# A graph layer and a layer of 64 experts on one core: the aggregation matrix from products of 32 by 128 instead of 64 by 64, thirteen instead of eleven experts' weights on chip, and a reordered transition and end

## The chip, the cores and the metric

The kernel runs on one core of a Trainium2 chip. A core has a matrix engine (TensorE, "PE" in the profile; "PEld" is its loading of weights, which overlaps it), a vector engine (VectorE, DVE), a scalar engine (ScalarE, ACT), a general engine (GpSimd, POOL) and a queue engine (SyncE, SP) that issues DMAs. Each works through its own instructions in order, and semaphores order them between engines. SBUF is the on-chip memory of 128 partitions, PSUM the accumulators that TensorE writes. The metric is the device time of one execution in microseconds: before the change 466.25 us, the median of three runs (465.24 to 466.73).

## The reference

There are 1024 tokens (nodes) of 512 values and 16384 edges sorted by destination.

```
x = x + relu(segment_sum(edge_val * (layernorm(x) @ W)[edge_col], edge_row) + bias)   # here row = src, col = dst
nx = layernorm(x)
scores = sigmoid(nx @ Wg.T + bg); w, idx = top_k(scores, 2); w = w / w.sum()           # 64 experts
h1 = (gamma_e * nx + beta_e) @ W1_e + b1_e      # 512 -> 256, per expert
h3 = (gamma_e * nx + beta_e) @ W3_e + b3_e
y  = sum over the two chosen experts of w_e * (silu(h1) * h3) @ W2_e + b2_e
z  = (silu(nxs @ Ws1 + bs1) * (nxs @ Ws3 + bs3)) @ Ws2 + bs2,  nxs = nx * gs + bs      # shared expert, width 32
out = x + y + z
```

Everything is fp32. The call passes the sorted `src` and `dst` in the edge places, as the first line is written above. The experts' matrices are 64 x 1.57 MB (W1, W3 and W2 of 512 KB each), some 100 MB that have to be read once.

## The kernel before, in words

**Graph layer.** The 1024 by 1024 aggregation matrix is built densely. The nodes of the sorted side are cut into 256 windows of DL = 4 nodes, in NH = 2 halves of 128 windows. A window's edges (up to 128, one a partition) are described by two one-hot matrices: one tells, for each edge, node-in-window times HI plus the high part of the other node's number, and the other, scaled by the edge's weight, its low part. With LO = 64 low and HI = 16 high values both have 64 columns, and their fp32 product (line 485) is the window's 64 by 64 piece of the matrix. NS = P / LO = 2 products go side by side into the two halves of the PSUM partitions. `one_hots` makes both one-hots for 16 windows, a group: VectorE compares (lines 398 and 400) and multiplies by the weight (401), ScalarE turns the first into fp32 (399). `matrix_group` makes the 16 products of a group and has ScalarE copy the accumulator, in two copies, into the tiles A (490). `turn` transposes A on TensorE (498), and ScalarE copies the result scaled by `sure` into AT (501). `weighted_sum` multiplies AT with the rows of layernorm(x) W (507). There are eight groups for each half; beside the second half's groups TensorE turns the first half's and begins the weighted sums of three tiles.

A fallback for edges that do not fit their window, in a branch, is not taken with these inputs, and its two loads of the flag (`unsure_i`) only hold up the engines a moment.

**Finishing and routing.** A loop over the 8 tiles of 128 tokens sums, normalizes, stores `nx_d` in device memory for the gathers, computes scores, chooses two experts (`choose`), ranks the tokens within each expert (`rank`, `put`) and marks slots and expert pairs (`slots`, `listed`). The result is `lists` and `tokens`: for each of 32 pairs of experts 64 + 64 slots with row numbers (691 and 692).

**Expert blocks.** 33 blocks: 32 expert pairs and, at place 24 of the order, a block for one expert's overflow beyond 64 tokens. The schedule is written by hand. For each block `gather` fetches 128 rows on POOL's queue (717), `scaled` transposes and applies gamma and beta (729, 731), `hidden` adds the biases by two pairs of bf16 matmuls (742: a pair for the high and middle terms and a pair for the low one) and does 16 fp32 matmuls for the pair, two experts side by side in the columns (746), then silu on ScalarE (749) and the product on VectorE (751), `turned`, `outputs` (768, 771), and a scatter of the block's 128 rows to `y_d` on POOL's queue (775). `outputs` of a block come after the hidden matmuls of the next one. Weights are loaded on SP's queue in the order W1, W3, W2 of each expert (703, 704, 706). They go to two rings of AHEAD = 11 slots: "w13" of 8 KB a partition and "w2" of 4 KB. Many tiles of the earlier stages are put in the same rings (`big` and `mid`: one-hots, A, AT), so that a weight load has to wait until the tile that had the slot is done with. Other tiles (rows, windows, transposed h) are in the pools `graph` and `graph2`.

Before the first block POOL zeroes four row buffers, four gathers are issued, and `weights` and the shared expert of two tiles (`other_rows`, `other_turn`, `other_sum`) are computed; the six other tiles follow from block 13 on. `beyond` and the functions after it make the overflow lists in blocks 2 to 12.

**End.** The last block is not scattered. `y_d` is read back in eight loads (1006) on the ACT and SP queues, the two rows of each token are multiplied by their weights and added to the result on VectorE (1014), and the last block's part comes from a one-hot matmul (`block_hots`, 1010) that VectorE adds (1016). Half of the first rows are added on TensorE with diagonal matrices instead.

## Time and profile before

| what | from | value |
|---|---|---|
| median of 3 runs | times | 466.25 us |
| the profiled execution | times | 467.33 us |
| its span, first to last instruction | page | 465.5 us |
| mean granted TensorE clock | page | 0.962 |
| busy: PE, PEld, DVE, ACT, POOL | page | 422.5, 210.6, 233.5, 112.0, 116.2 us |
| moved by DMA | page | 132.48 MB, 285 GB/s over the span |
| matrix phase, first to last product group | trace | 46.0 to 94.2 us |
| finishing loop's weighted sums end | trace | 165.4 us |
| first hidden matmul | trace | 191.2 us |
| last weights on chip | trace | about 431.8 us |

A profile is of one execution, and lies here 1.08 us above the median of the runs; 1.83 us of it are outside the span. A group of instructions is written as: line, engine, operation, output<-input, shape, count, then busy time, mean ns of one, and the idle time of the engine just before them with what ended it. A matmul that overlaps the next has a mean longer than its share of the time, so the pace is read from the starts. An fp32 matmul appears as two records with a weight load each. Times on POOL are rough.

### The profile page before, as it was taken

The page shows a single profiled execution, that of the slowest core. Times are in us where ns is not written, and L with a number is a line of the kernel's source. Part 1 is how long each engine was busy: PE and PEld are TensorE (multiplying, and loading weights), DVE is VectorE, ACT ScalarE, POOL GpSimd, SP SyncE. Part 2 cuts the span into 40 slices and gives each one's busy share as a digit, 9 for nine tenths or more (in the row PEclk, how much of TensorE's full clock was granted, in tenths as well). Part 3 has the DMA queues.
Part 4 walks back from the last instruction along what each step waited for, and adds up shares of the span by engine and source line. Part 5 has one row for each costly group of instructions (what it writes and reads, how often), then busy time and mean ns, then how long its engine had stood idle before and what let it go on. Part 6 is the DMA issues. An engine that isn't in the chain of part 4 may idle for free. (4 is left out here: it accounts for less than half of the span.)

```text
span 465.5 us, 6433 instructions
## 1 busy us (share of the span) xinstructions
PE 422.5 (91%) x2182; PEld 210.6 (45%) x2182; DVE 233.5 (50%) x690; ACT 112.0 (24%) x240; POOL 116.2 (25%) x148
## 2 busy tenths in 40 slices
PE   2999999987999964996999999999999999999781
PEld 1554996754555543332434434333333443434230
DVE  6879996036877875428424333233233232412265
ACT  1335785324121212011111212112121121212200
POOL 6542200000432124312223233232232322200200
PEclk9999999998999985799899999999999999999988
DMA  8286830360786195359999999999999999999194
GB/s 263 87 121 102 321 130 3 125 259 28 244 316 204 52 375 195 121 194 410 356 389 407 407 407 406 407 408 405 408 404 409 406 405 407 405 410 403 47 366 174
DMA packets 42294, 132.48 MB, mean 285 GB/s; under 512 B 8023, under 2 KB 8151, under 8 KB 42128
## 3 DMA queue, kind: packets, MB, share of 16 engines
q1 hardware_dynamic: 30464, 107.56, 59.7%
q0 software_dynamic: 8304, 18.17, 13.3%
q10 hardware_dynamic: 3488, 6.30, 3.7%
q8 instruction: 18, 0.29, 0.3%
q14 instruction: 20, 0.16, 0.1%
HBM read 124.00 MB, written 18.88 MB: 307 GB/s over the span
## 5 line engine op out<-in xcount | busy, mean ns | idle before, releaser
L746 PE MATMUL xph<-w,xT 128*64 128x512 f32 (+1 forms) x520 | 126.5, 602 | 0.9 <-DMA w<-in_L_ffn_W_dram 0.9
L775 POOL DMA_INDIRECT y_d<-xy,lists x31 | 31.9, 1030 | 169.8 <-ACT xhT L760 70.4
L746 PEld LDWEIGHTS xph<-w,xT 128*64 128x64 f32 (+1 forms) x520 | 39.0, 138 | 66.6 <-issue 63.6
L768 PE MATMUL xpy<-w,xhT 128*64 128x512 f32 (+1 forms) x260 | 67.0, 593 | 0.6 <-ACT xhT L760 0.6
L751 DVE TENSOR_TENSOR xh<-xa,xph 128x256 f32<-128x256 f32 x33 | 13.9, 421 | 106.8 <-ACT xa L749 106.8
L507 PE MATMUL acc<-hw,AT 128*128 128x512 f32 x128 | 61.5, 607 | 0.0
L749 ACT ACTIVATE xa<-xph 128x256 f32<-128x256 f32 x33 | 12.6, 383 | 152.1 <-PE xph L746 152.1
L717 POOL DMA_INDIRECT rows<-nx_d,tokens x32 | 35.5, 1109 | 12.4 <-issue 9.1
L768 PEld LDWEIGHTS xpy<-w,xhT 128*64 128x64 f32 (+1 forms) x260 | 21.5, 138 | 37.2 <-issue 35.1
L485 PEld LDWEIGHTS ph<-oh 128*64 128x64 f32 x512 | 31.7, 212 | 5.7 <-issue 3.3
L485 PE MATMUL ph<-oh 128*64 128x64 f32 x512 | 33.3, 302 | 0.1
L297 PE MATMUL ph<-w_sb,hT 128*128 128x512 f32 x64 | 30.5, 625 | 0.7 <-ACT hT L290 0.7
L771 ACT COPY xy<-xpy 128x512 f32<-128x512 f32 x33 | 19.3, 586 | 49.0 <-PE xpy L768 44.1
L729 DVE TENSOR_TENSOR xT<-xpt,gT 128x512 f32<-128x512 f32 x32 | 22.0, 687 | 16.7 <-PE xpt L194 15.3
L507 PEld LDWEIGHTS acc<-hw,AT 128*128 128x128 f32 x128 | 22.3, 193 | 17.4 <-issue 17.4
L731 DVE TENSOR_TENSOR xT<-xT,bT 128x512 f32<-128x512 f32 x32 | 22.2, 693 | 1.1
L607 POOL TENSOR_SCALAR so<-rank_at,here 128x128 f32<-128x128 f32 x14 | 8.9, 634 | 54.5 <-DVE here L598 54.5
L194 PE MATMUL xpt<-ident,rows 128*128 128x128 f32 x132 | 22.3, 296 | 0.0
L401 DVE TENSOR_TENSOR oh<-eq,wt 128x1024 f32<-128x1024 bf16 x16 | 19.6, 1224 | 3.6 <-PE pt L498 2.2
L194 PEld LDWEIGHTS xpt<-ident,rows 128*128 128x128 f32 x132 | 19.5, 211 | 1.1 <-issue 0.6
L758 PEld LDWEIGHTS xpht<-ident,xh 128*128 128x128 f32 x66 | 11.8, 216 | 16.1 <-DVE xh L751 7.0
L297 PEld LDWEIGHTS ph<-w_sb,hT 128*128 128x128 f32 x64 | 12.4, 203 | 14.1 <-issue 13.1
(275 smaller groups left out, 493.9 us busy)
## 6 DMA issues: line engine op xcount, KB each, us to landing
w<-in_L_ffn_W_dram SPq DMA_DIRECT2D x195, 512.0 KB
y_d<-zero POOLq DMA_DIRECT2D x1, 4096.0 KB
base_d<-in_L_gnn_bias_dram POOLq DMA_DIRECT2D x1, 2048.0 KB, 19.9
base<-base_d POOLq DMA_DIRECT2D x8, 256.0 KB, 13.3
nx_d<-nx ACTq DMA_DIRECT2D x8, 256.0 KB
ys<-y_d ACTq DMA_DIRECT2D x4, 512.0 KB
ys<-y_d SPq DMA_DIRECT2D x4, 512.0 KB
w_sb<-in_L_gnn_W_dram ACTq DMA_DIRECT2D x1, 1024.0 KB
```

The costliest lines, as they stand in the source:

```text
L194: nc.tensor.transpose(ps[:, k, :], v[:, k, :], ident[:n, :n])
L297: nc.tensor.matmul(ph, hT[:, k, :], w_sb[:, k, :], start=(k == 0), stop=(k == KC - 1))
L401: nc.vector.tensor_tensor(oh[:, 1], eq[:, 1], wt[:, h, None, q].to_broadcast([P, LO, 16]), ALU.mult)
L485: nc.tensor.matmul(pa[LO * w:LO * (w + 1), u, :], oh[:, 1, :, q], oh[:, 0, :, q], start=True, stop=True)
L507: nc.tensor.matmul(accs[t], ATs[h][t // 4][:, t % 4, wq, :], hws[h][:, wq, :], start=(h == 0 and wq == 0), stop=(h == NH - 1 and wq == NQ ...
L717: nc.gpsimd.indirect_dma_start(out=rows, out_offset=None, in_=nx_d[:, :], in_offset=bass.IndirectOffsetOnAxis(ap=of, axis=0), bounds_check ...
L729: nc.vector.tensor_tensor(xT.rearrange(view, n=n), pt.rearrange(view, n=n), g[:, :, :, None].to_broadcast(over), ALU.mult)
L731: nc.vector.tensor_tensor(xT.rearrange(view, n=n), xT.rearrange(view, n=n), b[:, :, :, None].to_broadcast(over), ALU.add)
L746: nc.tensor.matmul(ph[n * r:(n + 1) * r], xT[:, k, n * r:(n + 1) * r], w13[:, :, k, :], start=False, stop=(k == KC - 1))
L768: nc.tensor.matmul(py[n * r:(n + 1) * r], hT[:, c, n * r:(n + 1) * r], w2[:, c, :], start=(c == 0), stop=(c == HC - 1))
L771: nc.scalar.copy(y, py)
L775: nc.gpsimd.indirect_dma_start(out=y_d[:, :], out_offset=bass.IndirectOffsetOnAxis(ap=numbers, axis=0), in_=y, in_offset=None, bounds_chec ...
```

## The change

The line numbers of the kernel after differ, so parts are named by function.

1. `LO` becomes 32, so HI = 32 and NS = 4: a product is 32 by 128, and four go side by side. The first one-hot has 128 columns, of which ScalarE casts 96 and VectorE writes 32 directly; the second has 32 columns. `turn` transposes four contiguous slices. The window numbering follows.
2. `AHEAD` becomes 13. To make room, the pools `graph` and `graph2` give up most tiles to the two rings: three "w2" slots hold the ring of row tiles and one the transposed h until routing ends, and the overflow lists take one (`room`).
3. The biases become three bf16 terms stacked on 96 partitions, so that one pair of matmuls adds them; the loads of b1 and b3 become 12.
4. The routing chain: the bias matmul of the scores goes first, part of `put` goes to `choose`, the making of `rank_at` goes behind the matrix loop, `weights` goes behind the first block's hidden matmuls, all eight tiles' shared expert goes into the blocks from 6 on, ScalarE zeroes three row buffers in place of POOL's four, and three gathers are issued ahead.
5. The end: the last pair's W1 and W3 are loaded before its W2s; `y_d` is read back on SP's queue, issued ahead of the last block's hidden matmuls; the last two blocks are not scattered but added by one-hot matmuls, interleaved with the additions.

```
-AHEAD = 11
+AHEAD = 13
...
-    LO = 64
+    LO = 32
...
+    EH = E // 2
+    bias3 = const.tile([3 * EH, 2, 2 * H], BF16, name="bias3")
+    picks = const.tile([3 * EH, 2, E], BF16, name="picks")
...
+        row_ring = [pair[:, j] for pair in [mid([P, 2, D], "row", F32) for _ in range(3)] for j in range(2)]
+        turned_ring = mid([P, 2, KC, P], "hT", F32)
...
-                eq = mid([P, 2, LO, 16], "eq", BF16)
-                oh = big([P, 2, LO, 16], "oh")
-                nc.vector.tensor_tensor(eq[:, 0], iv, vl[:, 0, h, None, q].to_broadcast([P, LO, 16]), ALU.is_equal)
-                nc.scalar.copy(oh[:, 0], eq[:, 0])
-                nc.vector.tensor_tensor(eq[:, 1], iv, vl[:, 1, h, None, q].to_broadcast([P, LO, 16]), ALU.is_equal)
-                nc.vector.tensor_tensor(oh[:, 1], eq[:, 1], wt[:, h, None, q].to_broadcast([P, LO, 16]), ALU.mult)
-                return oh
+                v, low = vl[:, 0, h, None, q], vl[:, 1, h, None, q]
+                eq = mid([P, VA, 16], "eq", BF16)
+                ov = big([P, P, 16], "ov")
+                ol = mid([P, 2, LO, 16], "ol", F32)
+                eql = ol[:, 1].rearrange("p l q -> p (l q)").bitcast(BF16)[:, :LO * 16].rearrange("p (l q) -> p l q", q=16)
+                nc.vector.tensor_tensor(eq, iv[:, :VA], v.to_broadcast([P, VA, 16]), ALU.is_equal)
+                nc.scalar.copy(ov[:, :VA], eq)
+                nc.vector.tensor_tensor(eql, iv[:, :LO], low.to_broadcast([P, LO, 16]), ALU.is_equal)
+                nc.vector.tensor_tensor(ol[:, 0], eql, wt[:, h, None, q].to_broadcast([P, LO, 16]), ALU.mult)
+                nc.vector.tensor_tensor(ov[:, VA:], iv[:, VA:], v.to_broadcast([P, P - VA, 16]), ALU.is_equal)
+                return ov, ol[:, 0]
...
-                        nc.tensor.matmul(pa[LO * w:LO * (w + 1), u, :], oh[:, 1, :, q], oh[:, 0, :, q],
+                        nc.tensor.matmul(pa[LO * w:LO * (w + 1), u, :], ol[:, :, q], ov[:, :, q],
                                          start=True, stop=True)
...
+            def score_bias(t):
+                pls[t] = psh.tile([P, D], F32, name="ph")[:, :P]
+                nc.tensor.matmul(pls[t], ones[0:1, :], brow, start=True, stop=False)
...
             def bias_terms():
+                terms = mid([3 * EH, 2, 2 * H], "bterm", BF16)
+                v = b13.rearrange("p a m h -> p a (m h)")
+                for n in range(3):
+                    part = slice(n * EH, (n + 1) * EH)
+                    nc.vector.tensor_copy(terms, v)
+                    nc.vector.tensor_copy(bias3[part], terms[part])
+                    if n < 2:
+                        nc.vector.tensor_sub(v, v, terms)
...
-        for terms in (bias_hm, bias_lo):
-            rows = terms.shape[0]
+        for a in range(2):
             for n, (_, pick) in enumerate(parts):
-                nc.tensor.matmul(ph[n * r:(n + 1) * r], pick[:rows].to_broadcast([rows, r]), terms,
-                                 start=(terms is bias_hm), stop=False)
+                if a in pick:
+                    nc.tensor.matmul(ph[n * r:(n + 1) * r], pick[a].to_broadcast([3 * EH, r]), bias3[:, a, :],
+                                     start=(a == min(pick)), stop=False)
...
     def beyond():
+        room = wpool.tile([P, 16, E], F32, name="room", tag="w2")
...
-        for n in range(4):
+        for rows in rows_of:
+            nc.scalar.activation(rows, ones[:, 0:1].to_broadcast([P, D]), AF.Copy, scale=0.0)
+        for n in range(NR):
             fetch(n)
-        weights()
-        sts = [other_rows(i) for i in range(2)]
-        sTs = [other_turn(st) for st in sts]
-        for i in range(2):
-            other_sum(i, sTs[i])
         front(0)
+        fetch(NR)
         front(1)
...
+                if n < LAST:
+                    experts = [load_expert(nc.sync, W1[e:e + 1], W3[e:e + 1], W2[e:e + 1]) for e in both]
+                else:
+                    experts = list(zip([load_first(nc.sync, W1[e:e + 1], W3[e:e + 1]) for e in both],
+                                       [load_second(nc.sync, W2[e:e + 1]) for e in both]))
...
+            if n == LAST:
+                y_of = y_d.rearrange("(i p n) d -> i p n d", p=P, n=2)
+                ys = [wpool.tile([P, 2, 2, D], F32, name="ys", tag="w13")[:, j] for i in range(NT // 2) for j in range(2)]
+                for i in range(NT):
+                    nc.sync.dma_start(ys[i], y_of[i])
+                hots_last = [block_hots(tokens[:, NP - 2 + m:NP - 1 + m], w_last[m]) for m in range(2)]
             h = hidden(xTs.pop(n), parts)
-            back(n - 1)
+            if n < LAST:
+                back(n - 1)
+            else:
+                y_last = [outputs(*hTs.pop(LAST - 1))]
+            if n == 0:
+                weights()
...
-            if n >= 13 and (n - 13) // 3 + 2 < NT:
+            if n >= 6 and (n - 6) // 3 < NT:
...
+        add_block(0, 0)
+        y_last.append(outputs(*hTs.pop(LAST)))
+        add_block(0, 1)
+        for i in range(2):
+            add_rows(i)
+        for i in range(NT):
+            add_block(1, i)
+            if i + 2 < NT:
+                add_block(0, i + 2)
+                add_rows(i + 2)
+            add_sums(i)
```

`add_block(m, i)` is the one-hot matmul of the last but one (m = 0) or last block for tile i, `add_rows(i)` the two multiply-and-adds of tile i's rows read back, `add_sums(i)` the addition of the matmul's sum and the output DMA. For the last two tiles one of the two rows is added on TensorE with a diagonal matrix.

## The prediction

> **What bounds the kernel now.** I read first the page's slices of the span (each digit is a tenth; there are 40 slices of 11.6 us), then a table of windows cut at the stages, then inside each stage the groups of instructions, the waits of the load queue and, at the end, the chain of work that ended last.
>
> ```profile
> PE   2999999987999964996999999999999999999781
> PEclk9999999998999985799899999999999999999988
> DMA  8286830360786195359999999999999999999194
> ```
>
> ```profile
> 64.00:94.00 30.00, 30.00 (x281) 21.94 (x281) 13.57 (x21) 15.29 (x29) 0.00 (x0) 1.00 0.18 57
> 94.00:166.00 72.00, 68.09 (x271) 38.44 (x270) 50.29 (x224) 18.41 (x36) 15.45 (x27) 0.98 0.53 188
> 166.00:191.00 25.00, 15.02 (x56) 9.92 (x54) 15.95 (x78) 4.22 (x11) 11.01 (x17) 0.60 0.67 246
> 260.00:430.00 170.00, 169.38 (x801) 70.05 (x800) 54.86 (x131) 30.96 (x81) 46.44 (x43) 1.00 1.03 407
> 430.00:446.00 16.00, 11.65 (x42) 3.96 (x42) 2.66 (x10) 3.55 (x10) 3.14 (x4) 0.93 0.35 130
> ```
>
> Columns: window, length, busy time of PE, PEld, DVE, ACT and POOL, granted PE clock, DMA share, GB/s. To 166 us TensorE has no gap and DMA is mostly free: PE sets the time. From 166 to 191 routing ends and the first tokens are fetched: everything waits on a chain, at a clock of 0.60. From 260 to 430 both PE and DMA are full; the silu instructions, one a block, stand 6.9 to 7.7 us apart to 387 (PE's pace) and about 8 us from there. A block is 3.15 MB of weights, 7.7 us at 407 GB/s. So the last blocks wait for weights, and the end of the weight stream sets the end: PE waits last at 432.03, for a weight DMA. From 430 to the end a tail of 33.7 us (the last weights land at about 431.8) has neither engine full.
>
> **The matrix phase, 46 to 94 us.** Groups from the page, then ScalarE's from 46 to 94 us (busy us, mean ns, then idle before):
>
> ```profile
> L485 PEld LDWEIGHTS ph<-oh 128*64 128x64 f32 x512 | 31.7, 212 | 5.7 <-issue 3.3
> L485 PE MATMUL ph<-oh 128*64 128x64 f32 x512 | 33.3, 302 | 0.1
> ```
>
> ```profile
> L399 ACT CAST oh<-eq 128x1024 f32<-128x1024 bf16 x13 | 13.8, 1060 | 0.0
> L490 ACT COPY A<-ph 128x256 f32<-128x256 f32 x32 | 10.4, 376 | 18.4 <-PE ph L485 18.4
> L501 ACT ACTIVATE AT<-pt,sure 128x512 f32<-128x512 f32 x8 | 5.5, 688 | 0.0
> ```
>
> There are 16 groups of 32 matmul records. In the first half a group takes 1.9 to 2.0 us (45.98 to about 61.8 for eight), in the second 30 us / 8 = 3.75 us, of which the products are again 1.9 to 2.0, the turn 0.6, the weighted sums the rest. 32 records in 1.9 us are 59 ns a record. Weight loads of 128 columns start 109 to 121 ns apart, these of 64 columns 55 to 62: a load costs 0.85 ns a column. A full-clock matmul of 512 fp32 columns starts 430 ns after the one before, so 64 columns stream in 54 ns, and in 27 where two go side by side. So today's 59 ns is the load.
>
> After: a record loads 32 columns (27 ns) and streams 128 (107 ns, four side by side 27). 32 records give 0.87 us at best; I take 1.1, for the same tenth that today's loads run above their best and a start. Ends: 1.9 (issue binds, not the load) and 32 x 107 ns = 3.4 us (no two run side by side). 1.1 is nearest because the load row scales with columns in both forms that the trace has. PE would give back 0.8 x 16 = 13 us.
>
> ScalarE is late next. Its cast grows from 1024 elements (1.06) to 1536, by the same slope with 0.38 for 256 about 1.5; the two copies of A stay 0.65 and the turned copy 0.69. In order on ScalarE that is 2.15 us a group from 47.2 and 2.85 in the second half for the five groups that still have a cast, 1.34 for three: 47.2 + 17.2 + 14.2 + 4.0 = 82.6; PE by itself 46 + 9 to 15 + 8 x 2.9 ends between 80 and 84. VectorE makes a set of one-hots in 2.5 us as before (0.87 + 0.45 + 0.60 + 0.60, by the same rows, against 0.69 + 0.69 + 1.23), and has five sets of lead at 46 us. The loop ends at 84 for 94: **minus 10 us**, ends minus 14 and 0.
>
> The Trainium skill, "TensorEngine Tiling (Array Packing)", section Performance Considerations, speaks against the gain in two rules. It says that tiling makes the array faster but not the emptying of PSUM, and that after a fourfold gain the copy may bind; the 0.65 us of copies here is in line with that, and by it the phase would gain 10 us and not the 13 that PE gives back. It also warns that each matmul has some 60 cycles of overhead; if that were a floor for every record, a group would stay near 1.9 us and the phase gain nothing; no row here shows a record shorter than 55 ns.
>
> **Finishing loop, 98.7 to 165.4.** PE-bound at 9.8 us a tile, untouched but for the order: 0. The seven VectorE operations of rank_at moved behind the matrix loop (1.9 us at 34.8 to 36.7) lie beside PE work there; if that cover were gone they cost 1.9. Bias terms: 7 us of VectorE for 3.3, beside weighted sums: 0, at most +3.7. Twelve bias DMA issues in place of four on POOL, 0.52 each, put 4 us before the zeroing of y_d, whose first user is the first scatter near 200: 0.
>
> **End of routing to the first block.**
>
> ```profile
> 178.97 0.32 DVE L885 TENSOR_SCALAR st<-iota,expert,wts 128x64 f32<-128x64 f32 x1 [1.59 <-DMA nx_d<-nx]
> 179.22 2.03 POOL L713 MEMSET rows<- 128x512 f32 x4 [3.26 <-DMA w<-in_L_ffn_W_dram]
> 183.71 1.12 POOL L717 DMA_INDIRECT rows<-nx_d,tokens  x1 [2.46 <-DVE stt L887]
> ```
>
> In VectorE's strict order, weights() and other_rows stand between the last tile's ranks and the list, and wait 1.59 us for a DMA. Removed from that place: this wait and about 2 us of other work, so the token list, complete at 182.9, comes about 2 us sooner, and the gather, issued 0.8 us after it, about 2.5. The row zeroing goes to ScalarE, idle then. The transposes at 188.25 lose the matmuls of the other rows ahead of them. Together minus 4.5; but PE idles more before the first block, and half clock (0.50 from 180 to 190) stretches what follows. I take **minus 2.5**, ends minus 4.5 and 0 (gathers among the last preloads).
>
> **Weights held on chip.** Waits of the load queue from 170 to 235 us:
>
> ```profile
> SPq L703 <- PE xph L746: 20.8, 1, 20.8
> SPq L706 <- PE xpy L768: 12.7, 2, 7.1
> SPq L706 <- PE xpy L874: 8.0, 1, 8.0
> ```
>
> The queue stands until the first hidden matmuls free a slot (194.91), then until the first outputs (202.82), then twice more to 230. Today 11 experts are loaded before; after it 12 and two thirds, though the ring of second weights lends one slot to the overflow lists. Eleven plus the two matrices of the twelfth are there at 202.8 now, so at that point the lead is one expert, 1.57 MB / 407 GB/s = 3.9 us; while slots still bind (to 230) it may grow to two, 7.7. I take **minus 5.5**, ends minus 7.7 and minus 3.9. The preloads wait for slots of routing tiles: second weights of experts 8 to 12 for the last tile's row, its stored copy and its scores (about 163 to 172 now). If those hold the stream back past the first block, the gain is 0; that is a rival below.
>
> Bias products: one pair of 0.33 us starts in place of two, 0.33 x 32 = 10.6 us of PE in the loop. PE's pace to 387 has DMA just behind it, so this is worth nothing by itself: it keeps PE at some 7.0 us a block, below the 7.7 of the stream.
>
> **The end.**
>
> ```profile
> 432.03 0.20 PEld L746 LDWEIGHTS xph<-w,xT 128*64 128x64 f32 x4 [1.18 <-DMA w<-in_L_ffn_W_dram]
> 438.34 1.00 POOL L775 DMA_INDIRECT y_d<-xy,lists x1 [5.36 <-ACT xhT L760]
> ```
>
> ```profile
> 441.02 4.77 DMA ys<-y_d
> 445.81 0.76 DVE res L1014
> ```
>
> Now: weights land 431.8, the last scatter (block before last) is issued 6.5 us later and lands at 441.0, ys read back in 4.8, then 12 row additions of 0.76 and 8 sums of 0.69 on VectorE (14.9 us) and 4.8 us to the span's end. After: the last two blocks skip the scatter, so the last scatter is of a block one earlier, issued about when the last weights land and landing by T + 3 (2.7 us here; 6.1 is the median of all 31 under load, which is the other end). ys at T + 6 (bounds 5.5 and 11); VectorE 14 x 0.76 + 8 x 0.69 = 16.2, T + 22; then 4.8: T + 27 for T + 33.7. **Minus 6**, ends minus 9 (additions start under the last products) and minus 2. 18 products of 0.86 on PE lie beside VectorE's 16.2.
>
> **Sum.** -10 - 2.5 - 5.5 - 6 = -24. The profiled execution took 467.33 (span 465.5 and 1.83 around it), 1.08 above the median of the runs: 467.33 - 24 = 443.3, so a run at the median would take 442.3. I say 443.
>
> **Rivals.**
> 1. *Four products do not run side by side.* Place: the 16 groups. For: 128 columns stream twice as long as 64, and the trace has no 32-column form. Against: the 128*64 hidden matmuls have 520 records busy for 126.5 us, 243 ns each where 512 columns stream 430, so two do overlap. Price: +1.5 us x 16 = +24; the other terms give -14; result +10, **476**. It is slower than before from (14 / 16) + 1.9 = 2.8 us a group.
> 2. *The matrix phase gains nothing* (issue floor, or ScalarE's cast waits in line with the copies): -14, **453**. For: 18.4 us of ScalarE's idle time is all that the longer cast can use. Against: it needs only 13 casts x 0.45 = 6.
> 3. *Preloads stay behind the routing slots* and the lead is not there at the first block: -24 + 5.5, **449**.
> 4. *The read-back comes late* because the last scatter competes with the last weights: +5, **448**.
> 5. *ScalarE keeps up and the start shortens fully*: -14 - 4.5 - 6.4 - 6 = -31, **436**.
>
> **How the numbers follow.** Forecast 0.48; rival 1 0.10; rival 2 0.15; rivals 3 and 4 0.14 together; rival 5 0.10; several at once, ending within 0.3% of before (about what a measurement of this kernel can tell from no change) 0.02; slower by some other stall 0.01. Faster: 0.48 + 0.15 + 0.14 + 0.10 = 0.87; same 0.02; slower 0.11. The range takes all but rival 1 and the odd cases: 433 (a little below rival 5) to 459, where rivals 2 and 4 meet with part of each (-14 + 5 gives 457).
>
> **What the profile after would show.** Right: the group of ph<-ol,ov with 128*32 loads, 32 records in 1.0 to 1.2 us; the matrix loop ending near 84; ScalarE without idle time from 47 to 83; the first hidden matmul near 178; DMA share 1.0 from about 200; the last weights near 414; first additions of ys about 6 us later. Wrong: 3 us or more a group in the product rows (rival 1); a product group still 1.9 us, or PE waiting for ov (2); load-queue waits on rows, nx or hT past 180 (3); ys landing more than 10 us after the last weights (4).

## The result, and the profile after

The changed kernel takes 466.76 us (median of 20 runs, 465.67 to 468.65) against 466.41 us (20 runs beside it, 465.08 to 468.60): ratio 1.0009, with a 95% interval of 0.9996 to 1.0022. That is no change, where 443 was forecast with 433 to 459 around it. The profiled execution took 465.67 us, with a span of 463.9 and a granted clock of 0.964; against the profile before, the span is 1.6 us shorter, which is within the scatter of the runs (about 3 us from lowest to highest).

The slices of the span after (tenths busy, 40 slices of 11.6 us):

```profile
PE   2999999997999963987999999999998899999994
PEclk9999999998999975897999999999999999999998
DMA  8286580901687422299999999999999999999783
```

The table of windows after (window, length, busy time of PE, PEld, DVE, ACT and POOL, granted PE clock, DMA share, GB/s):

```profile
64.00:94.00 30.00, 30.00 (x284) 16.58 (x282) 22.28 (x45) 18.43 (x30) 0.00 (x0) 1.00 0.50 177
94.00:166.00 72.00, 68.75 (x278) 39.86 (x276) 50.52 (x225) 19.03 (x38) 16.32 (x29) 0.98 0.49 174
166.00:191.00 25.00, 13.91 (x54) 8.59 (x54) 12.71 (x58) 4.61 (x9) 7.84 (x10) 0.59 0.20 63
191.00:220.00 29.00, 22.90 (x113) 9.55 (x113) 17.77 (x52) 4.68 (x11) 7.15 (x7) 0.93 0.84 293
260.00:430.00 170.00, 161.59 (x725) 67.81 (x723) 54.00 (x128) 30.17 (x80) 45.55 (x45) 1.00 1.03 408
430.00:446.00 16.00, 15.76 (x59) 6.59 (x56) 10.70 (x29) 3.67 (x9) 1.04 (x1) 1.00 0.78 295
```

Three rows are to be read against the rows of before. In 64 to 94 TensorE is as full as it was, so the shorter products gave nothing back. From 166 to 191 the DMA share is 0.20 at 63 GB/s, where it was 0.67 at 246: 25 us in which weights were to be preloaded moved 1.6 MB instead of 6.2. From 260 to 430 PE has 7.8 us less work, which is the bias products' share, and the stream is as full as before.

**The matrix products.** Groups of the page after, then the timeline of PE for two product groups of after and two of before (start, length, instruction):

```profile
L487 PE MATMUL ph<-ov,ol 128*32 128x128 f32 x512 | 32.6, 415 | 0.1
L409 ACT CAST ov<-eq 128x1536 f32<-128x1536 bf16 x16 | 24.2, 1520 | 0.5 <-DVE eq L408 0.5
L487 PEld LDWEIGHTS ph<-ov,ol 128*32 128x32 f32 x512 | 23.5, 145 | 10.6 <-issue 4.4
```

```profile
72.67 2.13 PE L487 MATMUL ph<-ov,ol 128*32 128x128 f32 x32
...
89.57 2.18 PE L487 MATMUL ph<-ov,ol 128*32 128x128 f32 x32
```

```profile
72.84 2.27 PE L485 MATMUL ph<-oh 128*64 128x64 f32 x32
...
89.91 2.10 PE L485 MATMUL ph<-oh 128*64 128x64 f32 x32
```

A group still takes 2.1 us. In the seven groups of the second half that stand by themselves in both traces, a record starts 55 to 57 ns after the one before it, where before it was 57 to 64. The last group starts 0.3 us earlier. The cast is 1.52 us, as forecast, and hidden.

**The load queue.** Its longest wait from 170 to 235 us, its issues around it, and the one issue of ScalarE's queue that ends it:

```profile
SPq L725 <- DMA w_d<-wts: 23.7, 1, 23.7
```

```profile
173.20 0.33 SPq L732 DMA_DIRECT2D w<-in_L_ffn_W_dram  x1
197.22 0.33 SPq L725 DMA_DIRECT2D w<-in_L_ffn_W_dram  x1
197.60 0.63 SPq L726 DMA_DIRECT2D w<-in_L_ffn_W_dram  x1
```

```profile
192.77 0.38 ACTq L823 DMA_DIRECT2D w_d<-wts  x1
```

The queue stands for 24 us, and what it waits for is no slot and no engine. It is a store of 8 KB, `w_d`, which `weights` issues on another queue. The last load before the wait is W2 of the ninth expert; so nine experts are on chip when the first block runs, where the kernel before had eleven and thirteen were meant. In the trace's records the 226 DMAs of SP's and ScalarE's queues take eight completion semaphores strictly in turn, and none goes out before the one before it on the same semaphore has landed. W1 of the tenth expert has the same one as the store of `w_d`, which lands at 197.21; the load goes out at 197.22. Since `weights` moved behind the first block's hidden matmuls, this store is issued at 192.77 instead of 176.8.

The stores of `nx_d`, one for each tile of the finishing loop on ScalarE's queue, hold the loads in the same way. From 155 to 235 us there are also these waits of loads of W1 and W3, whose slots no row tile uses:

```profile
SPq L726 <- DMA nx_d<-row: 7.9, 1, 7.9
SPq L725 <- DMA nx_d<-row: 6.3, 1, 6.3
```

Only three loads are issued from 155 to 174 us, at 155.47, 163.71 and 173.20, each right behind such a store on its own semaphore. The store of `w_d` is the longest of these waits, not the only one.

**The end.** The chain of waits after, from its last weights on (start, length, what):

```profile
439.36 0.59 ACT xy L798
...
440.00 1.13 PE xpt L1046 x2
441.12 1.87 PE xpy L795 x8
442.99 1.06 PE xph L1046 x2
...
456.92 0.87 PE xpht L1046 x2
...
457.82 0.69 DVE res L1056
```

The last weight packet ends at 435.9, by the trace of the load queue, against 432.8 before (its first reading of 431.8 in the prediction was a little early). From there to the span's end it is 28.0 us for 32.7. Stage by stage:

| stage | before | after | change | forecast |
|---|---|---|---|---|
| start of the last product group | 89.91 | 89.57 | -0.3 | about -10 |
| first hidden matmul | 191.2 | 186.4 | -4.8 | -2.5 |
| load queue stands until | 194.91, 11 experts in | 197.22, 9 experts in | | 12.67 experts in |
| last weight packet | 432.8 | 435.9 | +3.1 | -18 |
| from there to the span's end | 32.7 | 28.0 | -4.7 | -6 |

The last two lines make up the -1.6 of the two profiled spans; the medians of the runs differ by +0.35.

### The profile page after: what moved, and what is told of

The parts are those of the page before. It is cut to its first block, busy times and chain, and to the rows that moved or that the text cites. A ratio compares the mean times of both kernels' runs of the same rounds, so it can differ in the third digit from the quotient of the medians.

```text
span 463.9 us, 6340 instructions
## 1 busy us (share of the span) xinstructions
PE 419.3 (90%) x2130; PEld 204.7 (44%) x2130; DVE 242.5 (52%) x723; ACT 119.9 (26%) x241; POOL 117.2 (25%) x153
## 4 chain that ended last, share of the span: by engine, by line
DMA 50%; PE 31%; DVE 4%; issue 2%; SPq 1%; ACT 1%; POOL 0%; ACTq 0%; POOLq 0%; DVEq 0%
DMA w<-in_L_ffn_W_dram 48%; PE acc L506 11%; PE ph L487 7%; PE xph L773 3%; PE pt L499 2%; PE ph L555 1%; PE xpy L795 1%; DMA w_d<-wts 1%; PE pt L193 1%; PE xpt L1046 1%; PE xph L1046 1%; PE xpht L1046 1%; PE xpy L1046 1%; DMA rows<-nx_d,tokens 1%; DVE bnst L166 0%
## 5 line engine op out<-in xcount | busy, mean ns | idle before, releaser
L773 PE MATMUL xph<-w,xT 128*64 128x512 f32 (+1 forms) x520 | 136.1, 606 | 8.2 <-DMA w<-in_L_ffn_W_dram 8.1
L773 PEld LDWEIGHTS xph<-w,xT 128*64 128x64 f32 (+1 forms) x520 | 44.7, 140 | 77.2 <-issue 72.4
L795 PE MATMUL xpy<-w,xhT 128*64 128x512 f32 (+1 forms) x260 | 74.2, 593 | 0.0
L795 PEld LDWEIGHTS xpy<-w,xhT 128*64 128x64 f32 (+1 forms) x260 | 23.9, 138 | 36.7 <-issue 33.9
L487 PE MATMUL ph<-ov,ol 128*32 128x128 f32 x512 | 32.6, 415 | 0.1
L487 PEld LDWEIGHTS ph<-ov,ol 128*32 128x32 f32 x512 | 23.5, 145 | 10.6 <-issue 4.4
L409 ACT CAST ov<-eq 128x1536 f32<-128x1536 bf16 x16 | 24.2, 1520 | 0.5 <-DVE eq L408 0.5
L193 PE MATMUL pt<-ident,row 128*128 128x128 f32 x64 | 12.0, 314 | 7.6 <-DVE row L187 2.8
```

What stands on the lines that cost most here:

```text
L193: nc.tensor.transpose(ps[:, k, :], v[:, k, :], ident[:n, :n])
L409: nc.scalar.copy(ov[:, :VA], eq)
L487: nc.tensor.matmul(pa[LO * w:LO * (w + 1), u, :], ol[:, :, q], ov[:, :, q], start=True, stop=True)
L773: nc.tensor.matmul(ph[n * r:(n + 1) * r], xT[:, k, n * r:(n + 1) * r], w13[:, :, k, :], start=False, stop=(k == KC - 1))
L795: nc.tensor.matmul(py[n * r:(n + 1) * r], hT[:, c, n * r:(n + 1) * r], w2[:, c, :], start=(c == 0), stop=(c == HC - 1))
```

## Experiments on the load queue

**The store on another queue.**

```
-        nc.scalar.dma_start(w_d.rearrange("(i p n) o -> p i (n o)", p=P, n=2), wts)
+        nc.gpsimd.dma_start(w_d.rearrange("(i p n) o -> p i (n o)", p=P, n=2), wts)
```

> Edit: only the DMA that stores the weights of the two chosen experts (w_d) goes from ScalarE's queue to GpSimd's, at the same place. Theory A (shared completion semaphore): in the kernel after, the load queue stands from 173.2 to 197.2 us because the load of W1 of the tenth expert uses the same one of eight DMA completion semaphores as this store, which is issued only after the first block's hidden matmuls. Then here the loads run on from 173, 12.67 instead of 9 experts are on chip at the first outputs (near 199), the lead of 3.67 experts is 14.2 us of stream at 407 GB/s, less 1.5 us that the next load waits longer: the last weights land 9 to 13 us earlier and the time is 454 to 458. Rival B (the loads wait for slots or for the DMA engines): nothing changes, 466 to 467.

Measured: 457.30 us against 466.16 (ratio 0.9797, 0.9772 to 0.9822). The queue's longest wait from 155 to 235 us, and its issues:

```profile
SPq L732 <- PE xpy L795: 20.9, 1, 20.9
```

```profile
174.90 0.33 SPq L725 DMA_DIRECT2D w<-in_L_ffn_W_dram  x1
...
181.69 0.33 SPq L726 DMA_DIRECT2D w<-in_L_ffn_W_dram  x1
204.02 0.33 SPq L732 DMA_DIRECT2D w<-in_L_ffn_W_dram  x1
```

The wait for `w_d` is gone. The queue runs on to 181.69 and then stands for a real reason, the slot that the first outputs free. At that point the loads of 12.67 experts are issued, the very number of the forecast, and the last weight packet ends at 428.9 instead of 435.9. So theory A holds: one store of 8 KB cost 9 us. What is new: the loads now run beside the first gathers, which land after 4.9 us in the median (2.8 in after), and the first hidden matmul goes back to 192.0 from 186.4.

**The store early, its queue unchanged.** `weights()` goes back ahead of the first block.

```
             fetch(n)
+        weights()
         front(0)
...
-            if n == 0:
-                weights()
```

> Edit: weights() (six small VectorE operations and the store of w_d on ScalarE's queue) goes back ahead of the first block, right behind the first three gathers; nothing else. Theory A: the store is issued near 180 and lands near 183, so the load queue stands 10 us instead of 24; the 3.67 experts that are left need 14.2 us and are on chip by about 198, still in time for the first outputs: within 1.5 us of the run with the store on GpSimd's queue, 454 to 459. Rival B: 466 to 467.

Measured: 459.58 us against 466.16 (0.9843, 0.9804 to 0.9882), 0.6 us above the range expected.

```profile
SPq L725 <- DMA w_d<-wts: 6.7, 1, 6.7
```

The wait for `w_d` is still there, but it is 17 us shorter than after's: the store is issued at 177.08, the queue resumes at 181.36, and the next stop ends at 204.01, as in the run above. Of the 9.5 us that the store's other queue brings, 7.2 come this way too.

**The store behind the first block's front.**

```
         front(0)
+        weights()
         fetch(NR)
...
-            if n == 0:
-                weights()
```

> Edit in the kernel after: weights() with its store on ScalarE's queue goes between the first block's scaling and the fourth gather, so that the store is issued near 187 and the load queue, which waits for it, stands until about 189.5: behind the first gathers, ahead of the first outputs. Theory A with contention (with the store on GpSimd's queue the preloads ran from 175 to 190 and the first gathers, in the same DMA engines, landed 5 us later, which put the first hidden matmuls at 192.0 instead of 186.4): here the first hidden matmuls come at 186 to 187, the preloads are done near 204 without a pause after them, and the time is 1 to 4 us below that run, 453 to 457. If the gathers' delay costs nothing (the stream sets the end), the time is the same, 457.

Measured: 461.01 us against 466.45 (0.9877, 0.9822 to 0.9932), 4 us above what was expected.

```profile
SPq L725 <- DMA w_d<-wts: 18.6, 1, 18.6
```

In this run the store is issued at 186.74 and the queue resumes at 191.82, where after has 192.77 and 197.22: with the run above, three kernels in which the load goes on 4.3 to 5.1 us after that store, wherever it stands. The queue is 5.4 us earlier, and the whole is 5.75 us shorter than after: those 5.4, and hardly more. The first hidden matmul is as early as after's, 186.0 for 186.4, but that earns nothing by itself. By 204 us this run has 11.4 experts on chip (counted from the queue's packets), the run with the store on GpSimd's queue 12.67; its stream ends 2.3 us later, at 431.2 for 428.9. Between these runs the position of the weight stream decides, not the start of the blocks.

**Eleven slots again, with the store out of the way.**

```
-AHEAD = 13
+AHEAD = 11
```

(and the `w_d` store on GpSimd's queue, as above)

> Edit on top of the store on GpSimd's queue: AHEAD 11 instead of 13, so that 10.67 instead of 12.67 experts are on chip at the first outputs (one slot still goes to the overflow lists). Forecast's term for the slots, by the stream: two experts are 7.7 us; the preloads are done sooner and collide less with the first gathers, which gives back up to 3: the time is 4 to 7 us above that run, 461 to 464. Rival (TensorE's pace, not the stream, sets the end by now): the same time, 457.

Measured: 467.73 us against 466.45 (1.0028, 0.9997 to 1.0060), that is 10.4 more than with 13 slots. Expected were 4 to 7. Two experts are 7.7 us of stream, and its second batch starts 1.5 later (205.47 for 204.02); the finishing loop, whose tiles share the rings, already ends 1.5 later (168.1 for 166.5). The two slots are thus worth more than the 5.5 of the prediction. Without them the stream ends at 438.6, later than the 432.8 of before, and the rest of the change only gives back at the end what it loses there.

**W1 and W3 of experts 8 to 12 ahead of their W2.** The idea: the second weights' slots are those that hold the routing's row tiles; the first weights' are free earlier.

```
+        first13, second = {}, {}
+        for e in range(8):
+            first13[e] = load_first(nc.sync, W1[e:e + 1], W3[e:e + 1])
+            second[e] = load_second(nc.sync, W2[e:e + 1])
+        for e in range(8, AHEAD):
+            first13[e] = load_first(nc.sync, W1[e:e + 1], W3[e:e + 1])
+        for e in range(8, AHEAD):
+            second[e] = load_second(nc.sync, W2[e:e + 1])
...
-                    experts = [load_expert(nc.sync, W1[e:e + 1], W3[e:e + 1], W2[e:e + 1]) for e in both]
+                    experts = [(first13[e], second[e]) if e in second else
+                               load_expert(nc.sync, W1[e:e + 1], W3[e:e + 1], W2[e:e + 1]) for e in both]
```

(and the `w_d` store on GpSimd's queue)

> Edit on top of the store on GpSimd's queue: on the load queue W1 and W3 of experts 8 to 12 go ahead of W2 of experts 8 to 12; those wait for the row tiles that routing gives back last (about 173), these for slots that are free by 165. Theory (preloads that run at 175 to 190 delay the first gathers by 5 us, and the stream then stands until 204): about 4 MB are loaded before 173, the rest of 2.5 MB by 181, all 13 experts are on chip, the first gathers land near 186, the first hidden matmuls come at 187 to 189, and the time is 3 to 7 us below that run, 450 to 454. If the delay of the gathers is not from the preloads: the same time, 457.

Measured: 453.44 us against 466.83 (0.9708, 0.9665 to 0.9751), as expected. It beats both kernels by 2.9%.

```profile
168.82 0.33 SPq L726 DMA_DIRECT2D w<-in_L_ffn_W_dram  x1
169.19 9.04 SPq L732 DMA_DIRECT2D w<-in_L_ffn_W_dram  x5
191.50 0.33 SPq L725 DMA_DIRECT2D w<-in_L_ffn_W_dram  x1
...
199.03 0.33 SPq L732 DMA_DIRECT2D w<-in_L_ffn_W_dram  x1
```

All first weights of the thirteen are issued by 168.82 and all second ones by 178.2 (thirteen experts for the 12.67 of the run with the store alone), ahead of the first gather at 180.4. The first hidden matmul is at 186.4 again, and its slots free the next loads at 191.50. The last weight packet ends at 422.6, 10.2 us earlier than before the change, and the tail is 28.7 us for 32.7.

That the slots of the second weights were what held the queue is not shown. In the run with the store on GpSimd's queue alone, loads of W1 and W3 wait for `nx_d` stores on their own semaphores, as in after:

```profile
SPq L725 <- DMA nx_d<-row: 9.0, 1, 9.0
SPq L726 <- DMA nx_d<-row: 7.2, 1, 7.2
```

In this run only one such wait is left from 155 us on, 2.7 us; the longer waits of the other loads of W1 and W3 are for slots that TensorE frees. The new order changed which load shares a semaphore with which store, and no run separates this from the slots.

## Experiments on the matrix products

**Each product as two of 64 columns.**

```
-                        nc.tensor.matmul(pa[LO * w:LO * (w + 1), u, :], ol[:, :, q], ov[:, :, q],
-                                         start=True, stop=True)
+                        for half in range(2):
+                            c = slice(64 * half, 64 * half + 64)
+                            nc.tensor.matmul(pa[LO * w:LO * (w + 1), u, c], ol[:, :, q], ov[:, c, q],
+                                             start=True, stop=True)
```

> Edit in the kernel after: each 32 by 128 product is made as two of 32 by 64, so that a group has 64 instead of 32 matmul records, each streaming half the columns; the result is the same. Theory M1 (a fixed cost of about 61 ns for each record): a group takes 3.9 us for 1.97, the matrix phase grows by 31 us, the time is about 497. Theory M2 (streaming binds, two of the four products side by side: 128 columns in 107 ns, half of it 53 ns a record): a group stays at 2.0 to 2.2 us and the time within 4 us of 466. Theory M3 (the load binds): a 32-column load at 0.85 ns a column is 27 ns, 64 of them 1.75 us: also about 2 us.

Measured: 477.58 us (one run; 466.16 before). The timeline of PE:

```profile
71.90 2.45 PE L489 MATMUL ph<-ov,ol 128*32 128x64 f32 x64
...
98.65 2.45 PE L489 MATMUL ph<-ov,ol 128*32 128x64 f32 x64
```

Twice the records in 2.4 us, starts 34 ns apart. A fixed price of 60 ns a record, M1, would give 3.9 us a group and is out. M2 and M3 gave 2.0 to 2.2 and are nearer. A record of 32 loaded columns can be issued in 34 ns, so in the changed kernel something else takes 56: it is something that grows with the streamed columns. The time itself was a miss for M2 and M3 (within 4 us of 466 expected): besides 0.3 us a group, TensorE stands idle 4.6 us in the matrix phase for nothing that the profile shows, and the last group starts 9.1 us later than after's. This was not followed further.

**Both one-hots in bf16.** One record a product instead of two.

```
-                ov = big([P, P, 16], "ov")
+                ov = big([P, P, 16], "ov").rearrange("p l q -> p (l q)").bitcast(BF16)[:, :P * 16].rearrange("p (l q) -> p l q", q=16)
...
-                nc.vector.tensor_tensor(ol[:, 0], eql, wt[:, h, None, q].to_broadcast([P, LO, 16]), ALU.mult)
+                olb = ol[:, 0].rearrange("p l q -> p (l q)").bitcast(BF16)[:, :LO * 16].rearrange("p (l q) -> p l q", q=16)
+                nc.vector.tensor_tensor(olb, eql, wt[:, h, None, q].to_broadcast([P, LO, 16]), ALU.mult)
```

(and the `w_d` store on GpSimd's queue)

> Edit on top of the store on GpSimd's queue: both one-hots of the products are bf16 (the edge weights are rounded), so that a product is one matmul record instead of two; ScalarE's cast of 1536 elements stays. Theory M1: 16 records of 61 ns, a group near 1.0 us. Theory M2: 128 bf16 columns in 53 ns, two side by side 27 ns a record, a group near 0.45 us. In both the forecast's matrix gain is tried in full: ScalarE binds the second half at 2.85 us a group, the matrix loop ends at 82 to 87 instead of 94, and the time is 7 to 12 us below the run with the store on GpSimd's queue.

Measured: 451.87 us against 466.16 (two runs; 0.9686, 0.9651 to 0.9720).

```profile
71.33 1.16 PE L488 MATMUL ph<-ov,ol 128*32 128x128 bf16 x16
...
84.27 1.16 PE L488 MATMUL ph<-ov,ol 128*32 128x128 bf16 x16
```

Sixteen records take 1.1 us, starts some 50 ns apart. Neither theory had that: the bf16 record is only a little cheaper than one of the two fp32 records. The time too was missed: 7 to 12 us below the run with the store moved alone were expected. But the run tells something else. The last group starts 5.3 us earlier than after's and is 1.0 shorter, and the kernel is 5.4 us faster than with the store moved alone (457.30). So what the matrix phase gains does reach the end, 5.4 us for 6.3. (The edge weights are rounded here, so this is a probe and not a rival kernel.)

**The streamed one-hot contiguous for each product.** In all layouts so far a window's columns lie 16 elements apart, 64 bytes in fp32, since the sixteen windows of a group are innermost. Here the tile of the streamed one-hot is laid out so that a product's 128 columns lie side by side.

```
-                ov = big([P, P, 16], "ov")
+                ov = big([P, 16, P], "ov").rearrange("p q l -> p l q")
```

(and the `w_d` store on GpSimd's queue)

> Edit on top of the store on GpSimd's queue: the 128-column one-hot is laid out so that the columns of one product are adjacent in memory (before, they stand 16 elements apart); VectorE and ScalarE write it with a stride instead. Seen so far, ns a record: 64+64 columns (load + stream) 59 to 61, 32+128 columns 61, 32+64 columns 37, 32+128 in bf16 68. Theory P (streams of side-by-side products share one path of about 0.42 ns a column, so that two fp32 streams fill it and four gain nothing more): a group stays at 1.95 us and the time within 2 us of the run with the store on GpSimd's queue, 455 to 459, or longer if the strided writes cost VectorE and ScalarE more. Theory S (the stride of 16 elements slows the reading): a group falls to 1.1 us or less, the matrix loop ends before 88.

Measured: 466.90 us against 466.45 (1.0004, 0.9973 to 1.0035). PE's timeline, the cast's group and PE's idle time, the last two from 40 to 104 us:

```profile
71.41 1.94 PE L487 MATMUL ph<-ov,ol 128*32 128x128 f32 x32 [1.39 <-ACT A L492]
...
79.69 1.11 PE L487 MATMUL ph<-ov,ol 128*32 128x128 f32 x32
...
97.92 1.11 PE L487 MATMUL ph<-ov,ol 128*32 128x128 f32 x32 [0.37 <-ACT A L492]
```

```profile
L409 ACT CAST ov<-eq 128x1536 f32<-128x1536 bf16 x16 | 48.9, 3070 | 0.0
L487 PE MATMUL ph<-ov,ol 128*32 128x128 f32 x512 | 23.7, 341 | 11.6 <-ACT A L492 11.3 <-PEq L438 0.3
L487 PEld LDWEIGHTS ph<-ov,ol 128*32 128x32 f32 x512 | 17.7, 153 | 21.1 <-ACT A L492 17.1 <-issue 1.6 <-ACT AT L500 0.8
```

This settles the products. With contiguous columns a group takes 1.04 us, starts 27 ns apart: the forecast's number. (In the windows of the groups of 1.94 us the granted clock is 0.50, in those of 1.11 it is 1.00.) Four do run side by side, and the 56 ns were the stride. But the price moves: the ScalarE cast writes with a stride now, each element 512 bytes from the one before, and takes 3.07 us for 1.52, and VectorE's part 1.13 for 0.68. ScalarE has no idle time left, its copies of A come late, PE waits for them, and the last group starts at 97.92. The kernel loses 9.6 us against the store moved alone.

**The same tile, written in order and read with the stride.**

```
-                nc.scalar.copy(ov[:, :VA], eq)
+                nc.scalar.copy(ov[:, :, :VA], eq.rearrange("p l q -> p q l"))
...
-                nc.vector.tensor_tensor(ov[:, VA:], iv[:, VA:], v.to_broadcast([P, P - VA, 16]), ALU.is_equal)
+                nc.vector.tensor_tensor(ov[:, :, VA:], iv[:, VA:].rearrange("p l q -> p q l"),
+                                        v.to_broadcast([P, P - VA, 16]).rearrange("p l q -> p q l"), ALU.is_equal)
```

(with the contiguous tile and the store as above)

> Edit on top of the store on GpSimd's queue: the 128-column one-hot again with a product's columns adjacent, and now ScalarE and VectorE also write in that order, so that their writes are contiguous and the stride is in what they read (bf16, 16 elements apart). With strided writes the cast took 3.07 us for 1.52, VectorE's part 1.13 for 0.60, and a group's products 1.04 us on TensorE at full clock. If the strided reading is free: cast 1.5, a group 1.05 us, ScalarE binds at 2.85 us a group in the second half as the forecast had it, the matrix loop ends at 84 to 88 instead of 94 and the time is 5 to 9 us below the run with the store on GpSimd's queue, 448 to 452. If reading with a stride costs what writing did: cast near 3, the loop ends near 100 and the time is 464 to 468.

Measured: 470.86 us against 466.83 (1.0076, 1.0038 to 1.0114).

```profile
L409 ACT CAST ov<-eq 128x1536 f32<-128x1536 bf16 x16 | 50.2, 3142 | 0.0
```

To read bf16 with a stride of 16 elements (32 bytes) costs ScalarE the same as to write fp32 with one of 128 (512 bytes). Here too ScalarE pays for the turn of the axes, and it has no room for it.

**That layout with the best load order.** The edits of the two runs "first halves ahead" and "contiguous, written in order" together.

> Both edits: contiguous one-hot columns written in order, and W1 and W3 of experts 8 to 12 ahead. The two gains lie one behind the other on the path, so they should add: if both hold, 442 to 449; if only one of the edits gains alone, that one's time within 2 us.

Measured: 464.99 us against 466.83 (0.9954, 0.9919 to 0.9989), 11.5 more than the load order alone. This was a miss: it expected at least the time of one of the edits, but the contiguous layout loses whatever stands behind it.

**The kernel before with one operand contiguous, and with both.** Both from the kernel before, with the streamed 64 columns laid side by side; in the second, the 64 loaded columns too.

```
+                ov = oh[:, 0].rearrange("p l q -> p (l q)").rearrange("p (q l) -> p l q", q=16)
+                ol = oh[:, 1]
...
-                nc.scalar.copy(oh[:, 0], eq[:, 0])
+                nc.scalar.copy(ov, eq[:, 0])
...
-                nc.vector.tensor_tensor(oh[:, 1], eq[:, 1], wt[:, h, None, q].to_broadcast([P, LO, 16]), ALU.mult)
-                return oh
+                nc.vector.tensor_tensor(ol, eq[:, 1], wt[:, h, None, q].to_broadcast([P, LO, 16]), ALU.mult)
+                return ov, ol
```

> Edit in the kernel before: the 64 columns that a product streams stand next to one another in memory instead of 16 elements apart (ScalarE's cast writes them with a stride); the 64 columns that it loads as weights keep their stride. The prediction took the load for the limit of today's 59 ns a record (0.85 ns a column). If the load is the limit: a group of 32 records on TensorE at full clock stays at 1.9 us. If the strided streaming is: it falls to 1.1 to 1.8 us, the nearer to 1.1 the less the load counts.

> Edit in the kernel before: both operands of a product, streamed and loaded, contiguous (VectorE and ScalarE write with a stride). If the stride of the loaded columns slows the load: a group falls below that of the run with only the streamed columns contiguous, down to 0.9 us at 27 ns a record; if loads do not care for the stride: the same as there.

Measured: 469.06 us with one and 465.31 with both, beside one run of before at 468.45; these are single runs and are read for their traces alone. PE's timeline of the first, then of the second:

```profile
71.84 2.01 PE L487 MATMUL ph<-oh 128*64 128x64 f32 x32
```

```profile
74.47 1.15 PE L487 MATMUL ph<-oh 128*64 128x64 f32 x32
...
87.38 1.15 PE L487 MATMUL ph<-oh 128*64 128x64 f32 x32
```

With only the stream contiguous a group stays at 2.0 us, 58 ns a record: in the kernel before it was indeed the load that bound. With the loaded columns contiguous as well it falls to 1.08 us, 30 ns a record. So the strided load of 64 columns costs about twice the contiguous one. In this run ScalarE's cast takes 2.02 us for 1.06, and the last group still starts 2.5 us earlier than before (87.38 for 89.91).

## Why the prediction was wrong, point by point

**The matrix phase** (forecast -10, measured 0). The step that failed is "streams 128 (107 ns, four side by side 27)". The step before it, that the load bound the kernel before, held: 58 ns with a strided load of 64 columns beside a contiguous stream, 30 with both contiguous. That its price of 0.85 ns a column agreed with the loads of 128 columns was chance: loads of 128 contiguous columns (`so` of the slot lists) start 110 ns apart too, yet 64 contiguous columns, two products side by side, take at most 30 ns a record, 0.47 a column. The streaming price was taken from full-clock matmuls of 512 contiguous columns, and the streamed one-hot has its columns 64 bytes apart. A strided stream of 128 columns costs some 56 ns with four products side by side. The change halved the load and put a stream of the same length in its place. No row of the trace showed such a stream by itself, but the code did: the index `q`, which a product fixes, is the innermost of both one-hot tiles. The Trainium skill, "SBUF — State Buffer", section "Door 1: The DMA port swizzle", says that SBUF has 16-byte lines and that each access that goes to a new line pays a penalty, so that only a stride within 4 fp32 values is free. The falls from 56 to 27 ns and from 58 to 30 agree with it; no run here tried a stride that short.

The size of the term was too large besides. In the bf16 run, whose groups take the forecast's 1.1 us, the last product ends at 85.4 us for 92.0, 6.6 earlier and not 10: in the second half TensorE is full, and groups start 2.6 to 3.45 us apart where the prediction had 2.85 to 2.9.

Rival 2 gave the right price for this part (0 instead of -10) but for other causes: neither an issue floor (27 ns a record was reached) nor ScalarE's cast (1.52 us, hidden) held it. Rival 1 was wrong: four products do run side by side. A floor near 1.9 us a group, which the prediction drew from 60 cycles of overhead a matmul (32 records of 60 ns, so a cycle of 1 ns, which no run shows), is not there: 1.04 us was measured.

**The end of routing to the first block** (forecast -2.5, bounds -4.5 and 0; measured -4.8). Of the 4.8, 0.5 are the finishing loop's earlier end (164.8 for 165.3). The mechanism was right, but the size was helped by the fault of the load queue: with the store moved alone the loads run beside the first gathers and the first hidden matmul is at 192.0, a little past the prediction's worse bound; only with the other load order as well is it at 186.4 again. And the term was added to the sum as if it shortened the whole. The run with `weights` behind the first block's front has the same early first block and gains only what the load queue gains, so this term is worth hardly anything by itself; it counts through the slots that it frees.

**Weights held on chip** (forecast -5.5; measured, with the store's wait, the last weights 3.1 us later). The mechanism was right: with the wait gone, two slots are worth 10.4 us, and 12.67 experts are on chip at the first stop. The step that failed is the move of `weights` in the paragraph before it, "Removed from that place: this wait and about 2 us of other work". `weights` also issues a store on ScalarE's queue, and that store was counted at nothing. It shares a completion semaphore with a weight load, and moved 16 us later it held the load queue for 24 us. Rival 3 had the effect, a lead that is not there, but named the slots of routing tiles as the cause, and its price ended at no gain; what came was a loss, since the queue had nine experts at 197 us where the kernel before had eleven at 195. The trace of before had a sign that was passed over: between 165 and 171 us a load of W3 waits 4.5 us for a store of `nx_d`, on the other queue and from a tile that shares no buffer with the weights there. From 95 us on such waits for `nx_d` come to 45 us in that trace, the longest 23.0.

**The bias products** (forecast 0). Right: 7.8 us less PE work from 260 to 430, while the stream paces that stretch at 1.03 in both kernels.

**The end** (forecast -6, measured -4.7). Nearly right in size: the forecast had 27 us from the last weights to the end, measured are 28.0, and the tail before was 32.7 and not the 33.7 that it read. The last scatter is issued at 433.57, ahead of the last weights, and the read-back begins 3.2 us later at 436.80. What came late was another engine: the 18 additions on PE, 0.86 us each, were put "beside VectorE's 16.2". They begin at 440.0 with the last block's outputs among them, end at 457.8, and are what the chain goes through.

**The sum.** Rivals 2 and 3 came together, and the third with a loss. Without the matrix part the prediction's terms gave -14 and 453; the kernel with the store and the load order put right takes 453.44. That is chance in part: the load order is no part of the change, and with the store alone put right it is 457.30, a gain of 9 for 14. The parts are not the forecast's either: 10.2 us came from the stream (forecast 8) and 4.0 from the end (forecast 6).

## What to carry to other kernels

Price a TensorE operand by its layout as well as its column count: read the innermost stride of both operands in the code, and take a duration only from a row with the same stride. When a step is moved, list each DMA it issues and ask what else waits for that DMA's completion; with semaphores in rotation this includes loads that have nothing to do with its data, on other queues too. A gain before a stream-bound stage is worth what it adds to the stream's position, in bytes on chip at a given time; in these runs an earlier first block alone added hardly anything.

## What the runs showed of the hardware

- A matmul record whose fp32 columns lie 64 bytes apart takes about twice a contiguous one, on either side: 58 for 30 ns with 64 columns loaded, 56 for 27 ns with 128 streamed four side by side. Halving the streamed columns with the stride kept gives 34 ns.
- One bf16 pass over 128 columns 32 bytes apart (starts 50 ns apart) is hardly cheaper than one fp32 pass over columns 64 bytes apart (56). Under these strides the type of the data saved only the second pass.
- ScalarE and VectorE slow down by 1.6 to 2.1 when the axes are turned, whether they write fp32 512 bytes apart or read bf16 32 bytes apart: a cast of 1536 elements takes 3.07 and 3.14 us for 1.52, a compare of 512 elements 1.13 and 1.11 for 0.68.
- One store of 8 KB on one queue stopped another queue for 24 us, through a completion semaphore used by both (the store lands at 197.21, the load goes out at 197.22); putting it on GpSimd's queue was worth 9.5 us.
